# Layer 3's end, run as three stages in turn, against one walk in which shaping, convolutions and closing go side by side

## The chip, the cores and the metric

The kernel runs on one core of a Trainium2 chip. A core has TensorE (PE in the profile, with its weight loads shown apart as PEld), VectorE (DVE), ScalarE (ACT), GpSimd (POOL) and SyncE (SP), each with an instruction queue of its own; transfers are started from these queues and moved by 16 DMA engines. The metric is the device time of one execution in microseconds; a kernel's time is the median of its runs.

## What is computed

The network applies four layers to x of shape (4, 96, 56, 56) in float32: attention, a selective scan, a windowed mixture, and the layer of this change. Each layer's output is added to its input. Only the end of layer 3 matters here. Up to that point the layer has made `xz = in_proj(x)`, split in two halves of 192 channels, and four cumulative results `y` (rows, rows backwards, columns, columns backwards). The rest is, cut to its core:

```python
y1, y2 = y[:, 0], y[:, 1, :, ::-1]
y3, y4 = ...                      # the two column orders, turned back to row order
ys = y1 + y2 + y3 + y4            # each with its Ds added
mu, var = yn.mean(-1), yn.var(-1) # over 192 channels
yn = (yn - mu) / jnp.sqrt(var + 1e-05) * ln_g + ln_b
u = jnp.moveaxis(yn, -1, 1) * z   # z: second half of in_proj(x)
t = relu(bn(conv2d(u, c1_w)))                     # 1x1, 192 -> 384 channels
t = relu(bn(conv2d(t, c2_w, groups=384, pad=1)))  # 3x3, one filter per channel
t = conv2d(t, c3_w, c3_b)                         # 1x1, 384 -> 96 channels
s = relu(t.mean((2, 3)) @ se1_w.T + se1_b)
s = sigmoid(s @ se2_w.T + se2_b)
return t + t * s[:, :, None, None]
```

## The kernel before

An image has L = 3136 positions. They are taken in 7 chunks of 448 columns (8 image rows; `NCH`, `CH`), or in 28 groups of 112 positions (`KT`, `NKT`), four of which make a chunk. The 384 channels are three tiles of 128 (`NM`, index m). The four batches are called b.

`layer3` (L1516) first runs `into_layer3` and `cumulative`; neither is touched by the change, apart from the number of taps that `convolve` now gets with each tile. What follows them is the stage of this case. Its weights are loaded on SP's queue, the two batch norms are turned into scale and shift (L1543 and after), and then the loop over b (L1649 to L1659) does three things for one batch, and only then goes to the next batch:

1. Shaping, `gathered` (L1554). Per chunk it loads the four y tiles, 112 positions x 4 x 192 channels (L1565, L1571, all on SP's queue, three buffers of each), adds them and Ds on VectorE (L1575, L1576), normalises in `norm_rows` (L768: statistics L773 and L774, square root on ScalarE L776, reciprocal L778, subtract and scale L780, times gamma L784, plus beta L785), computes z by four matmuls with `wz` (L1581), multiplies (L1582), and turns the result by eight transposes (L1586) so that channels lie on partitions; ScalarE copies the halves into g (L1590).
2. Bottleneck, `convolve` (L386). It walks tiles and chunks; in one step it convolves chunk c of the tile before and fills chunk c of the next tile. A fill is two matmuls with c1 (L1601) and one ScalarE activation (L1605) into a padded image. The nine taps of the 3x3 filter are split: `on_pe` = 4 are matmuls with a diagonal matrix (L413, diagonals made at L399), which accumulate in PSUM; the other five are VectorE instructions on the same PSUM tile (L418); ScalarE's `ended` (L1611) writes the result to t2.
3. Closing. Seven times three matmuls with c3 (L1627) and an activation that also sums (L1628), then the mean (L1632, L1633), se1 (L1635, L1637), se2 with its sigmoid (L1639, L1641), and seven outputs `o` = t3 x gate + x (L1646), each written by a DMA from GpSimd's queue (L1647). x was loaded for the whole batch at L1594.

PSUM has eight banks: three for fills, turned halves and c3 (`op`), two for z (`oz`), three for the convolutions (`od`). The pools of SBUF are opened anew for every batch. The bottleneck's convolutions are issued `in_order`: the instructions of each engine run in the order in which the program writes them. Elsewhere a scheduler may move them.

Of the kernel before, what the change touches and what calls it, by code (L numbers as in the profile page):

```python
# [9 lines left out]
F32 = mybir.dt.float32  # L10
# [7 lines left out]
L = H * W  # L18
CH = 448
# [50 lines left out]
class Net:  # L70
# [315 lines left out]
    def convolve(self, tiles, two, sp, ps):  # L386

        nc = self.nc  # L390
        on_pe = 4
        for j in range(len(tiles) + 1):
            now = tiles[j] if j < len(tiles) else None
            old = tiles[j - 1] if j > 0 else None
            if now is not None:
                now["xp"] = two[j % 2]
                dg = now["dg"] = sp.tile([128, on_pe, 128], F32, name="dg")
                for k in range(on_pe):
                    nc.vector.tensor_scalar(  # L399
                        dg[:, k, :], self.ident, now["weights"][:, k : k + 1], None, ALU.mult  # L400
                    )
            for c in range(NCH):
                if old is not None:
                    xp, w = old["xp"], old["weights"]

                    def tap(k):
                        y = 8 * c + k // 3
                        return xp[:, y : y + 8, k % 3 : k % 3 + W]

                    p = ps.tile([128, 512], F32, name="d")  # L410
                    q = p[:, :CH].rearrange("p (h w) -> p h w", w=W)
                    for k in range(on_pe):
                        nc.tensor.matmul(q, old["dg"][:, k, :], tap(k), start=k == 0, stop=k == on_pe - 1)  # L413
                if now is not None:
                    now["fill"](c, now["xp"][:, 1 + 8 * c : 9 + 8 * c, 1 : W + 1])
                if old is not None:
                    for k in range(on_pe, 9):
                        nc.vector.scalar_tensor_tensor(q, tap(k), w[:, k : k + 1], q, ALU.mult, ALU.add)  # L418
                    old["ended"](c, q)

    def into_scan(self, xin, dram, orders):
# [7 lines left out]
        with ExitStack() as cx:  # L429
# [19 lines left out]
            def tile_of(pr, j):  # L449
# [46 lines left out]
                return dict(weights=cw[:, j, :], fill=fill, ended=ended)  # L496
# [594 lines left out]
    def into_layer3(self, xin, dram):  # L1091
# [4 lines left out]
        with ExitStack() as cx:  # L1096
# [19 lines left out]
            def tile_of(pr, j):  # L1116
# [41 lines left out]
                return dict(weights=cw[:, j, :], fill=fill, ended=ended)  # L1158
# [357 lines left out]
    def layer3(self, xin, xout, dram):  # L1516
# [4 lines left out]
        with ExitStack() as cx:  # L1521
            wp = cx.enter_context(tc.tile_pool(name="ow", bufs=1))
            ga = cx.enter_context(tc.tile_pool(name="og", bufs=1))
            ps = cx.enter_context(tc.tile_pool(name="op", bufs=3, space=PSUM))
            psz = cx.enter_context(tc.tile_pool(name="oz", bufs=1, space=PSUM))
            psd = cx.enter_context(tc.tile_pool(name="od", bufs=3, space=PSUM))
            wz = wp.tile([C, DI], F32, name="wz")
            nc.sync.dma_start(wz, self.d["l3_win"][:, DI : 2 * DI])

            lng, lnb, ds = (self.load_rows(wp, n) for n in ("l3_lnw", "l3_lnb", "l3_d"))  # L1530
            dsum = wp.tile([KT, DI], F32, name="dsum")
# [22 lines left out]
            def gathered(b, g, sp, ss):  # L1554

                xn = sp.tile([C, L], F32, name="xn")
                nc.sync.dma_start(xn, xs[b])
                for t0 in range(0, NKT, 4):
                    four = [KT, 4, DI]
                    yk = []  # L1560
                    for k in range(4):
                        y = ss.tile(four, F32, name=f"y{k}")
                        if k < 2:
                            src = ys[k][b, t0 * KT : (t0 + 4) * KT, :].rearrange("(t p) d -> p t d", p=KT)
                            nc.sync.dma_start(y, src)  # L1565
                        else:
                            for r in range(2):
                                src = ys[k][b].rearrange("(w h) d -> w h d", h=H)[
                                    :, 2 * t0 + r : 2 * t0 + r + 7 : 2, :
                                ]  # L1570
                                nc.sync.dma_start(y[r * W : (r + 1) * W], src)  # L1571
                        yk.append(y)
                    acc = yk[0]
                    for k in (1, 2, 3):
                        nc.vector.tensor_tensor(acc, acc, yk[k], ALU.add)  # L1575
                    nc.vector.tensor_tensor(acc, acc, spread(dsum, 4), ALU.add)  # L1576
                    self.norm_rows(acc, lng, lnb, ss)
                    z = psz.tile([KT, 4, 256], F32, name="z")
                    for i in range(4):
                        at = (t0 + i) * KT  # L1580
                        nc.tensor.matmul(z[:, i, :DI], xn[:, at : at + KT], wz, start=True, stop=True)  # L1581
                    nc.vector.tensor_tensor(acc, acc, z[:, :, :DI], ALU.mult)  # L1582
                    for dh in range(2):
                        p = ps.tile([128, 512], F32, name="pn")
                        for i in range(4):
                            nc.tensor.transpose(  # L1586
                                p[:96, i * KT : (i + 1) * KT], acc[:, i, 96 * dh : 96 * dh + 96],
                                self.ident[:KT, :KT],
                            )
                        nc.scalar.copy(g[:, dh, t0 * KT : (t0 + 4) * KT], p[:96, : 4 * KT])  # L1590

            def bottleneck(b, g, sp, s1, ss):
                x = s1.tile([C, L], F32, name="x")
                nc.sync.dma_start(x, xin[b])  # L1594
                t2 = s1.tile([128, NM, L], F32, name="t2")

                def tile_of(m):
                    def fill(c, dst):
                        p = ps.tile([128, 512], F32, name="pn")
                        for dh in range(2):  # L1600
                            nc.tensor.matmul(  # L1601
                                p[:, :CH], c1[:, dh, m * 128 : (m + 1) * 128],
                                g[:, dh, c * CH : (c + 1) * CH], start=dh == 0, stop=dh == 1,
                            )
                        nc.scalar.activation(  # L1605
                            dst, p[:, :CH].rearrange("p (h w) -> p h w", w=W),
                            AF.Relu, bias=s1h[:, m : m + 1], scale=s1c[:, m : m + 1],
                        )

                    def ended(c, p):  # L1610
                        nc.scalar.activation(  # L1611
                            t2[:, m, c * CH : (c + 1) * CH], flat(p),
                            AF.Relu, bias=s2h[:, m : m + 1], scale=s2c[:, m : m + 1],
                        )

                    return dict(weights=c2[:, m, :], fill=fill, ended=ended)

                two = self.padded(s1)
                with in_order(tc):
                    self.convolve([tile_of(m) for m in range(NM)], two, sp, psd)  # L1620
                t3 = s1.tile([C, L], F32, name="t3")
                sums = ss.tile([C, NCH], F32, name="sums")
                for c in range(NCH):
                    cs = slice(c * CH, (c + 1) * CH)
                    p = ps.tile([128, 512], F32, name="pn")
                    for m in range(NM):
                        nc.tensor.matmul(p[:C, :CH], c3[:, m, :], t2[:, m, cs], start=m == 0, stop=m == NM - 1)  # L1627
                    nc.scalar.activation(  # L1628
                        t3[:, cs], p[:C, :CH], AF.Identity, bias=c3b, accum_out=sums[:, c : c + 1]
                    )  # L1630
                mean = ss.tile([C, 1], F32, name="mean")
                nc.vector.tensor_reduce(mean, sums, AX.X, ALU.add)  # L1632
                nc.vector.tensor_scalar(mean, mean, 1.0 / L, None, ALU.mult)  # L1633
                p = ps.tile([128, 512], F32, name="pn")
                nc.tensor.matmul(p[: DI // 4, 0:1], se1, mean, start=True, stop=True)  # L1635
                h1 = ss.tile([DI // 4, 1], F32, name="h1")
                nc.scalar.activation(h1, p[: DI // 4, 0:1], AF.Relu, bias=se1b)  # L1637
                p = ps.tile([128, 512], F32, name="pn")
# [4 lines left out]
                for c in range(NCH):  # L1643
                    cs = slice(c * CH, (c + 1) * CH)
                    o = ss.tile([C, CH], F32, name="o")
                    nc.vector.scalar_tensor_tensor(o, t3[:, cs], gate, x[:, cs], ALU.mult, ALU.add)  # L1646
                    nc.gpsimd.dma_start(xout[b][:, cs], o)  # L1647

            for b in range(B):  # L1649
                g = ga.tile([96, 2, L], F32, name="g")  # L1650
                with ExitStack() as c2x:
                    sp = c2x.enter_context(tc.tile_pool(name="ob", bufs=1))
                    ss = c2x.enter_context(tc.tile_pool(name="os", bufs=3))
                    gathered(b, g, sp, ss)
                with ExitStack() as c2x:
                    sp = c2x.enter_context(tc.tile_pool(name="tb", bufs=2))
                    s1 = c2x.enter_context(tc.tile_pool(name="t1", bufs=1))
                    ss = c2x.enter_context(tc.tile_pool(name="ts", bufs=3))
                    bottleneck(b, g, sp, s1, ss)  # L1659
# [141 lines left out]
```

## Time and profile before

| | |
|---|---|
| median of 4 runs | 16304.19 us (16290.62 to 16332.49) |
| the profiled execution | 16290.62 us, span 16288.5 us |
| PE busy over the span | 13211.2 us (81%) |
| PEld | 8975.2 us (55%) |
| DVE | 13644.1 us (84%) |
| ACT | 12217.7 us (75%) |
| POOL | 7905.3 us (49%) |
| mean granted TensorE clock | 0.919 |
| the stage of the change | from about 15465 us to the end at 16288.5 us |

The page cuts the span into 40 slices; the stage is a little more than the last two of them. In these rows each digit is the busy share, or the granted clock, of one slice in tenths:

```profile
PE   8999977777777777777777678788888888888876
DVE  8666559999999999999998766678888888888866
ACT  0555449999999999999997255488888888888822
POOL 0000048888888888888886022133333333333300
PEclk7999989999999999999998588888999999999977
```

In the last two slices no engine is close to full, ScalarE is at two tenths and GpSimd at nought, and the clock is at seven tenths. A share of busy time over a slice of 407 us covers several batches' stages, so the stage has to be read in windows that follow these stages. The times of a group of instructions are recorded per instruction; a float32 matmul leaves two records.

### The profile page before, as it was taken

What the parts mean: (1) busy time and instruction counts of PE and PEld (TensorE: products, weight loads), DVE (VectorE), ACT (ScalarE), POOL (GpSimd) and SP (SyncE); (2) the same over time, 40 slices, a digit from 0 to 9 for tenths busy, and PEclk for the clock granted to TensorE, in tenths of its full rate; (3) what the DMA queues carried; (4) which work ended last, traced back from release to release, by engine and by line L of the source; (5) the groups of instructions that cost most, each with busy time, mean ns of one, the idle gap of its engine ahead of it and who ended that gap; (6) DMA issues with size and microseconds to landing.
All of it is one profiled execution on the core that took longest, in us unless ns stands there. A gap on an engine that the chain in (4) does not pass through costs nothing.

```text
span 16288.5 us, 501766 instructions
## 1 busy us (share of the span) xinstructions
PE 13211.2 (81%) x222032; PEld 8975.2 (55%) x222032; DVE 13644.1 (84%) x15363; ACT 12217.7 (75%) x15540; POOL 7905.3 (49%) x4079
## 2 busy tenths in 40 slices
PE   8999977777777777777777678788888888888876
PEld 4333336666666666666665555456666566666543
DVE  8666559999999999999998766678888888888866
ACT  0555449999999999999997255488888888888822
POOL 0000048888888888888886022133333333333300
PEclk7999989999999999999998588888999999999977
DMA  0000043333444433434445800221212221222122
GB/s 15 1 1 4 14 157 92 92 92 93 105 105 104 104 93 93 94 94 104 104 106 124 213 17 10 78 50 49 51 48 51 51 50 48 51 50 51 43 67 64
DMA packets 821406, 1152.54 MB, mean 71 GB/s; under 512 B 309360, under 2 KB 728720, under 8 KB 807456
## 3 DMA queue, kind: packets, MB, share of 16 engines
q1 hardware_dynamic: 759872, 1055.38, 26.5%
q10 hardware_dynamic: 53984, 45.77, 1.2%
q8 instruction: 1746, 28.61, 0.8%
q0 software_dynamic: 5376, 19.27, 0.4%
q14 instruction: 428, 3.51, 0.1%
HBM read 842.93 MB, written 277.18 MB: 69 GB/s over the span
## 4 chain that ended last, share of the span: by engine, by line
PE 34%; DVE 28%; ACT 21%; issue 11%; DMA 4%; POOL 1%; SPq 0%; ACTq 0%; DVEq 0%; POOLq 0%
DVE q L634 17%; PE q L1427 7%; ACT ht L659 5%; ACT e L622 4%; PE s L233 4%; PE d L413 3%; ACT phi L1375 3%; PE z L1367 3%; DVE w L1415 3%; PE acc L251 2%; PE m L196 2%; PE y L671 2%; ACT w L1383 2%; PE t L557 2%; PE t L650 2%
## 5 line engine op out<-in xcount | busy, mean ns | idle before, releaser
L614 POOL TENSOR_TENSOR q<-du,bm 128x1792 f32<-128x1792 f32 x1344 | 5348.7, 4026 | 3.1 <-DMA bm<-bc 3.1
L634 DVE TENSOR_TENSOR_SCAN q<-e,state,q 128x448 f32<-128x448 f32 x4608 | 4875.0, 1123 | 143.5 <-ACT e L622 137.3
L622 ACT ACTIVATE e<-dl,na 128x448 f32<-128x448 f32 x5376 | 3354.6, 640 | 173.2 <-DVE q L634 118.3
L671 PE MATMUL y<-ht,cd 128*32 128x64 f32 x75264 | 1839.2, 225 | 1468.9 <-ACT ht L659 1466.8
L650 PE MATMUL t<-ident,q 128*128 128x128 f32 x18816 | 2618.1, 293 | 94.0 <-issue 77.9
L1427 PE MATMUL q<-w,m 32*32 32x192 f32 x52224 | 2582.4, 348 | 118.3 <-DVE phi L1436 68.6
L650 PEld LDWEIGHTS t<-ident,q 128*128 128x128 f32 x18816 | 2382.7, 203 | 324.4 <-issue 200.9
L659 ACT COPY ht<-t 128x896 f32<-128x896 f32 x2688 | 2428.7, 904 | 91.5 <-PE t L650 60.7
L671 PEld LDWEIGHTS y<-ht,cd 128*32 128x32 f32 x75264 | 1402.3, 110 | 1947.8 <-ACT ht L659 1930.2
L1427 PEld LDWEIGHTS q<-w,m 32*32 32x32 f32 x52224 | 1878.0, 113 | 731.5 <-issue 162.2
L1436 DVE TENSOR_TENSOR phi<-q,phi 128x768 f32<-128x768 f32 x1632 | 1513.8, 953 | 547.3 <-PE q L1427 524.8
L1448 POOL TENSOR_TENSOR t<-t 128x384 f32<-128x384 f32 x408 | 407.2, 998 | 2999.5 <-DVE t L1447 2999.5
L1367 PE MATMUL z<-ad,sm 32*32 32x256 f32 x39168 | 1277.7, 391 | 397.0 <-ACT phi L1375 383.7
L1375 ACT COPY phi<-z 128x1536 f32<-128x1536 f32 x816 | 1164.9, 1428 | 536.2 <-PE z L1367 536.0
L241 ACT ACTIVATE e<-s 128x896 f32<-128x896 f32 (+1 forms) x1050 | 922.0, 915 | 846.9 <-PE m L196 505.0
L208 DVE TENSOR_REDUCE pm<-m 128x1 f32<-128x448 f32 (+1 forms) x1700 | 997.7, 618 | 618.9 <-PE m L196 574.2
L1415 DVE TENSOR_TENSOR w<-w,misc 128x3072 f32<-128x3072 f32 x408 | 1365.4, 3347 | 83.1 <-PE misc L1399 46.3
L1383 ACT ACTIVATE w<-phi,lntiny,w_k_rmask 128x3072 f32<-128x3072 f32 x408 | 1203.0, 2949 | 2.6
L1391 ACT ACTIVATE phi<-phi,w_k_nmask 128x3072 f32<-128x3072 f32 x408 | 1165.6, 2857 | 2.4
L196 PE MATMUL m<-ka,qa 32*128 32x448 f32 (+1 forms) x3400 | 1135.2, 614 | 8.6 <-DVE pm L208 7.5
L1367 PEld LDWEIGHTS z<-ad,sm 32*32 32x32 f32 x39168 | 709.8, 105 | 659.3 <-ACT phi L1375 469.3
L292 POOL DMA_DIRECT2D x<-xc x28 | 14.5, 517 | 2080.6 <-DVE xc L291 2079.6
(254 smaller groups left out, 18703.0 us busy)
## 6 DMA issues: line engine op xcount, KB each, us to landing
bm<-bc SPq DMA_DIRECT2D x896, 448.0 KB
cm<-cd SPq DMA_DIRECT2D x544, 186.0 KB
l1y<-out SPq DMA_DIRECT2D x672, 96.0 KB
l1y<-out SPq DMA_DIRECT2D x672, 72.0 KB
y<-l1y ACTq DMA_DIRECT2D x224, 168.0 KB
l3y<-y SPq DMA_DIRECT2D x1616, 23.2 KB
w<-l3cr SPq DMA_DIRECT2D x408, 48.0 KB
l3cr<-phi SPq DMA_DIRECT2D x408, 48.0 KB
```

The costliest lines, as they stand in the source:

```text
L614: nc.gpsimd.tensor_tensor(q, spread(s["du"][:, j, :], ng), s["bm"][g], ALU.mult)
L622: nc.scalar.activation(e[:, :CH], s["dl"][:, j, :], AF.Exp, scale=na[:, s["k"], j, n : n + 1])
L634: nc.vector.tensor_tensor_scan(a, e, a, first, ALU.mult, ALU.add)
L650: nc.tensor.transpose(flat(t)[:, 128 * c : 128 * c + 128], view(q, h * NC2 + c, [[NC, 128]]), self.ident,)
L659: nc.scalar.copy(t, flat(s["t", j, g, h])[:, : NC2 * 128])
L671: nc.tensor.matmul(s["y", j][r : r + 32, c // 4, 64 * half : 64 * half + 64], s["cd"][:, half, g, c, :], s["t", j, g, h][:, 128 * i + 64 * ...
L1367: nc.tensor.matmul(z[32 * b : 32 * b + 32, p, dh].rearrange("p n d -> p (n d)"), s["s"][ps_, dh, b, lo : lo + 32], st["ad"][ps_, dh, 8 * h ...
L1375: nc.scalar.copy(st["phi"][:, :, :, 8 * h : 8 * h + 8, :].rearrange("p a b n d -> p a b (n d)"), z.rearrange("p a b n d -> p a b (n d)"),)
L1383: nc.scalar.activation(w.rearrange("p a n d -> p (a n d)"), st["phi"].rearrange("p a b n d -> p (a b n d)"), AF.Sigmoid, bias=lntiny, scal ...
L1415: nc.vector.tensor_tensor(st["w"], st["w"], ut, ALU.mult)
L1427: nc.tensor.matmul(qp[bs, n, :DI], st["m"][bs, 4 * q + n, :], st["w"][bs, :, 4 * q + n, :], start=True, stop=True,)
L1436: nc.vector.tensor_tensor(ph, view(st[q], 0, [[256, 4], [32, 6], [1, 32]]), ph, ALU.mult)
```

## The change

Everything at the end of layer 3 is issued in one walk, in program order on every engine.

- `gathered(b)` becomes a generator that yields three times per chunk, and is cut into parts: `fetch` (loads, issued three chunks ahead at first and two ahead later; xn per chunk), `added`, `statistics` (with the square root on ScalarE), `normalised` (z matmuls, reciprocal, and the subtraction and scaling as four ScalarE Identity activations per chunk), `gated` (multiplication by z) and `turned`. Gamma is folded into the weight of z (`wg`), beta into a second one (`wz`), whose product with xn is accumulated by one 448-column matmul before four plain matmuls with the identity that turn the chunk.
- For the first batch, the additions stay on VectorE, and the loads of y1 and y3 go to ScalarE's queue. For the other three the additions are GpSimd's and all y loads SP's.
- `convolve` is called once, for all 12 tiles of the four batches, and calls `before()` ahead of a step and `beside()` behind it. `beside` advances the shaping of the next batches by one yield, `before` the closing of the batch before. So 13 slots of 7 steps are walked, 91 steps.
- `closing(b)` is a generator that starts in the 21(b+1)th step: one c3 chunk per step, then residual loads (seven on ScalarE's queue, in seven buffers `o`) with the mean, se1, se2 with the gate, one output per step.
- The taps on TensorE are 3, 2 and 3 for the three tiles instead of 4.
- PSUM: two banks for fills and c3 (`op`), two for z, one for the turned halves (`ot`), three for convolutions.

```diff
-    def convolve(self, tiles, two, sp, ps):
+    def convolve(self, tiles, two, sp, ps, before=lambda: None, beside=lambda: None):
...
             for c in range(NCH):
+                before()
                 if old is not None:
-                    xp, w = old["xp"], old["weights"]
+                    xp, w, on_pe = old["xp"], old["weights"], old["on_pe"]
...
                     old["ended"](c, q)
+                beside()
...
-            ps = cx.enter_context(tc.tile_pool(name="op", bufs=3, space=PSUM))
+            ps = cx.enter_context(tc.tile_pool(name="op", bufs=2, space=PSUM))
             psz = cx.enter_context(tc.tile_pool(name="oz", bufs=1, space=PSUM))
+            pst = cx.enter_context(tc.tile_pool(name="ot", bufs=1, space=PSUM))
             psd = cx.enter_context(tc.tile_pool(name="od", bufs=3, space=PSUM))
...
+            wg = wp.tile([C, DI], F32, name="wg")
+            nc.vector.tensor_tensor(wg, wz, lng[:C], ALU.mult)
+            nc.vector.tensor_tensor(wz, wz, lnb[:C], ALU.mult)
...
+            def fetch(b, c):
...
+                for k in range(4):
+                    y = ss.tile(four, F32, name=f"y{k}", bufs=3)
+                    queue = nc.sync if b > 0 or k % 2 == 0 else nc.scalar
...
+            def added(q):
+                y = q["ys"]
+                engine = nc.gpsimd if q["b"] > 0 else nc.vector
+                engine.tensor_tensor(y[0], y[0], y[1], ALU.add)
+                engine.tensor_tensor(y[2], y[2], y[3], ALU.add)
+                engine.tensor_tensor(y[0], y[0], y[2], ALU.add)
+                engine.tensor_tensor(y[0], y[0], spread(dsum, 4), ALU.add)
+
+            def statistics(q):
...
+                for i in range(4):
+                    nc.vector.bn_stats(st[:, i, :], acc[:, i, :])
+                    nc.vector.bn_aggr(mv[:, i, :], st[:, i, :])
+                rs = q["rs"] = ss.tile([KT, 4], F32, name="rs")
+                nc.scalar.activation(rs, mv[:, :, 1], AF.Sqrt, bias=self.eps[:KT])
+
+            def normalised(q):
...
+                for i in range(4):
+                    nc.tensor.matmul(
+                        z[:, i, :DI], q["xn"][:, i * KT : (i + 1) * KT], wg, start=True, stop=True
+                    )
+                nc.vector.reciprocal(rs, rs)
+                nm = ss.tile([KT, 4], F32, name="nm")
+                nc.vector.scalar_tensor_tensor(nm, mv[:, :, 0], -1.0, rs, ALU.mult, ALU.mult)
+                for i in range(4):
+                    nc.scalar.activation(
+                        acc[:, i, :], acc[:, i, :], AF.Identity,
+                        bias=nm[:, i : i + 1], scale=rs[:, i : i + 1],
+                    )
+
+            def gated(q):
+                acc = q["ys"][0]
+                nc.vector.tensor_tensor(acc, acc, q["z"][:, :, :DI], ALU.mult)
+
+            def turned(q):
...
+                for dh in range(2):
+                    p = pst.tile([128, 512], F32, name="tr")
+                    nc.tensor.matmul(
+                        p[:96, :CH], wz[:, 96 * dh : 96 * dh + 96], q["xn"], start=True, stop=False
+                    )
                     for i in range(4):
...
+                        nc.tensor.matmul(
+                            p[:96, i * KT : (i + 1) * KT], acc[:, i, 96 * dh : 96 * dh + 96],
+                            self.ident[:KT, :KT], start=False, stop=i == 3,
+                        )
+                    nc.scalar.copy(gs[b][:, dh, c * CH : (c + 1) * CH], p[:96, :CH])
+
+            def gathered(b):
+                qs = [fetch(b, c) for c in range(3)]
+                added(qs[0])
+                for c in range(NCH + 1):
+                    if c < NCH:
+                        statistics(qs[c])
+                    if c > 0:
+                        turned(qs[c - 1])
+                        if c + 2 < NCH:
+                            qs.append(fetch(b, c + 2))
+                    yield
+                    if c == NCH:
+                        return
+                    normalised(qs[c])
+                    if c + 1 < NCH:
+                        added(qs[c + 1])
+                    yield
+                    gated(qs[c])
+                    yield
...
+                return dict(weights=c2[:, m, :], on_pe=(3, 2, 3)[m], fill=fill, ended=ended)
...
+            def closing(b):
...
+                yield
                 for c in range(NCH):
...
+                    yield
+                os = []
+                def residual(c):
+                    o = ss.tile([C, CH], F32, name="o", bufs=7)
+                    nc.scalar.dma_start(o, xin[b][:, c * CH : (c + 1) * CH])
+                    os.append(o)
+                for c in range(NCH):
+                    residual(c)
...
+                    yield
+                    o = os[c]
+                    nc.vector.scalar_tensor_tensor(o, t3[:, cs], gate, o, ALU.mult, ALU.add)
                     nc.gpsimd.dma_start(xout[b][:, cs], o)
...
+            def ending():
+                for b in range(B):
+                    coming = closing(b - 1) if b > 0 else iter(())
+                    for _ in range(NM * NCH):
+                        next(coming, None)
+                        yield
+                yield from closing(B - 1)
+
+            ends = ending()
+            outputs = (x for b in range(1, B) for x in gathered(b))
+            with in_order(tc):
+                for _ in gathered(0):
+                    pass
+                self.convolve(
+                    [tile_of(b, m) for b in range(B) for m in range(NM)], two, sp, psd,
+                    lambda: next(ends, None), lambda: next(outputs, None),
+                )
+                for _ in ends:
+                    pass
```

## The prediction

> **What bounds the kernel now.** The change touches only the last 823 us of the span (15465 to 16288.5), so I read the windows of that stretch first, then its groups, the timeline, and windows of 3.41 us that lie on the clock's own grid.
>
> In the windows the columns after the bounds are length, busy time of PE, PEld, DVE, ACT, POOL, granted clock, DMA share and GB/s.
> ```profile
> 15465.00:15553.00 88.00, 32.73 (x116) 27.39 (x117) 66.00 (x161) 10.62 (x24) 0.78 (x8) 0.52 0.58 141
> 15553.00:15668.00 115.00, 110.47 (x295) 54.21 (x293) 74.55 (x115) 37.22 (x59) 0.52 (x1) 0.99 0.03 7
> 15668.00:15692.00 24.00, 2.87 (x8) 2.31 (x8) 9.42 (x19) 0.05 (x1) 3.09 (x7) 0.50 0.88 225
> 15692.00:15751.00 59.00, 26.69 (x105) 23.66 (x106) 57.23 (x135) 9.61 (x21) 0.00 (x0) 0.56 0.44 113
> ```
> Batch 0 is shaped in 88 us with DVE bound (clock 0.52), convolved and closed in 115 with PE full (0.99); batch 1 then waits 24 us for loads. The cycle, about 203 us, repeats four times. Over all of it PE is busy 573 us and DVE 568 of 823: most of what one does, the other stands beside.
>
> In the groups (busy, mean ns, idle before and its releasers) and two spots of the timeline:
> ```profile
> L418 DVE SCALAR_TENSOR_TENSOR d<-xp,w_l_c,d 128x448 f32<-128x448 f32 x420 | 287.4, 689 | 125.8 <-PE d L413 108.7 <-ACT t L1611 3.4
> L413 PE MATMUL d<-xp,dg 128*128 128x448 f32 x672 | 263.1, 538 | 0.0
> L1605 ACT ACTIVATE xp<-pn,bn_sh,bn_sc 128x448 f32<-128x448 f32 x84 | 61.1, 727 | 131.5 <-PE pn L1601 131.5
> ```
> ```profile
> 15777.70 3.66 DVE L418 SCALAR_TENSOR_TENSOR d<-xp,w_l_c,d 128x448 f32<-128x448 f32 x5 [0.86 <-PE d L413]
> 15776.88 0.73 ACT L1611 ACTIVATE t<-d,bn_sh,bn_sc 128x448 f32<-128x448 f32 x1 [1.46 <-DVE d L418]
> 15839.05 0.72 ACT L1611 ACTIVATE t<-d,bn_sh,bn_sc 128x448 f32<-128x448 f32 x1 [2.77 <-DVE d L418]
> ```
> Each 448-column f32 matmul is two records 0.376 us apart: 0.752. A step of four taps on PE plus fill is 6 x 0.752 = 4.51, while DVE's five taps take 3.66 (0.725 each): PE waits for nothing, DVE for PE.
> ```profile
> 4208.30:4211.71 3.41, 2.48 (x16) 1.71 (x14) 3.41 (x3) 3.37 (x6) 1.56 (x1) 1.00 0.70 152
> 4211.71:4215.12 3.41, 1.52 (x58) 1.27 (x59) 3.41 (x4) 3.41 (x6) 3.41 (x2) 0.99 0.00 0
> 4215.12:4218.54 3.42, 3.42 (x35) 3.09 (x36) 3.42 (x5) 2.66 (x6) 3.42 (x2) 0.51 0.08 19
> 15748.78:15752.19 3.41, 2.74 (x10) 2.22 (x11) 1.90 (x8) 1.06 (x2) 0.78 (x8) 0.50 0.06 11
> 15752.19:15755.60 3.41, 3.41 (x6) 1.50 (x5) 0.00 (x0) 0.73 (x1) 0.00 (x0) 0.50 1.00 258
> 15759.02:15762.43 3.41, 3.41 (x10) 1.71 (x9) 0.00 (x0) 1.45 (x2) 0.00 (x0) 1.00 0.00 0
> ```
> One window with PE 45% busy (1.52) halves the clock in the next; a cold window 80% busy (2.74) leaves it cold; after a full one (3.41) it is full again by 15759.
>
> **The change, part by part.** Program order holds on each engine, so I follow each queue; "step" is one chunk of one tile, 91 in all: 7 that only fill, 77 that fill and convolve, 7 that only convolve.
>
> Fewer taps on PE: (3,2,3) gives DVE 6, 7, 6. DVE's step is 6 x 0.725 = 4.35 or 5.05, PE's (with two fill matmuls) 3.76 or 3.01: DVE bounds a plain step where PE did.
>
> Shaping beside the steps. Per chunk on DVE: statistics 4 x (0.340 + 0.174) = 2.06, overlapped about 1.95; reciprocal and product 0.35 (L778 has 0.173 each); gating 0.96 (L1582, 0.941). Sum 3.26; 7 chunks over 3 tiles, 7.6 per tile. Removed: L780, L784, L785 and, for batches 1 to 3, the additions (L1575, L1576). GpSimd's additions: L1005 has 1.605 for 112x672 and 1.842 for 112x784, so 1.81 for 112x768, 7.2 per chunk, hidden behind the step and a half before their statistics; bare, 7.2 x 20 = 145. ACT's four Identities (112x192) lie between L945 (112x96, 0.363) and L1628 (96x448, 0.630): 0.46, nearer the first in size, 1.6 with their overlap, hidden under the step's taps; bare 1.6 x 21 = 34. PE gets four z matmuls (L1581: eight records in 2.77 at half clock, so about 1.3) and two 448-column ones for the folded lnb (1.5) per chunk: 2.8 x 7 = 20 a batch, under DVE's lead of 1.3 to 2.0 a step where no bubble stands. The folding itself is two products of 0.36 at the start.
>
> The new wait. In 19 of the conv steps (3 turns when the chunk's three steps fall so in a tile, else 2; only one in the last, at step 65) DVE's taps are followed by statistics, ACT's square root waits for these, and the copy of the first half of `turned` stands behind the root. With one bank for `tr`, PE's second half waits for that copy, and the next convolution is queued behind it on PE. From the end of statistics DVE is idle for root 0.30 (L776), copy 0.53 (L1590), second half 0.75 + 4 x 0.20 = 1.57 (two records each, 0.10 by L1030's ten in 1.01), next three taps 2.26, handovers 0.6: 5.3 us (4.6 with two taps). What is late next is the whole following step: its taps, `ended`, and the fill of the next tile. With root and copies in the other order it would be nothing; that is the lower bound, the upper one adds the half clock (below).
>
> Closing beside tile 2's steps. c3's third matmul needs `ended` of the step before and stands ahead of the next convolution, so the step is a chain: conv 2.26, gap 0.16, taps 4.35, `ended` 0.72, c3 0.75, handovers 0.25: 8.5. Shaping fits into it, bar about 5 per `turned`. It replaces 7 x 2.26 of bare closing per batch.
>
> Queues. SP gets the y and xn loads two chunks ahead and only them; each waits for its buffer, and nothing else stands behind it. POOL's output DMAs (L1647, 0.51) stand behind its additions, with seven `o` buffers nobody waits for them. Residual loads: 7 issues at 0.31 to 0.34 (L834) on ACT, which stands until y loads in flight land (1.55 MB at 225 GB/s, 6.9 us); mostly hidden, 3 us x 3. With all cover gone 7 x 3.
>
> First batch: nine y loads move to ACT's queue ahead of the bn roots. SP keeps the rest, weights between y parts; DVE's bn work stands between the additions. Chunk 0's sums I put at 29.5 us (now its statistics start at 23.7); bounds 23.7 and 24 + 2 x 6.9 = 38. Then a chunk is a chain over ACT, PE and DVE: root 0.3, copy 0.53, second half at half clock 3.1, copy 0.53, four Identities 1.6, gating 0.96, statistics 1.95, six handovers of 0.2: 10.2 (the copies on ACT are 8.72 apart at present, and DVE's own work, additions 3.9 + 3.26, is 7.2). Four such, two of 9.2 where the turn is missing or early, a last turn of 6 and 7 to the first fill: 102 (now 85.5, from 15465 to the first fill). The 7 fill-only steps: 10.5 + two turns x 4.7 = 20.
>
> Sum at full clock: seven steps of 4.35 (30.5), 5.05 (35.4) or 8.5 (59.5) per tile, shaping 7.6, bubbles, outputs (L1646, 0.70 each, steps 11 to 17 of the next batch), ACT's 3:
> - batch 0: 30.5 + 7.6 + 2 x 5.3 = 48.7; 35.4 + 7.6 + 2 x 4.6 = 52.2; 59.5 + 2 x 5 = 69.5; together 170
> - batch 1 (three turns in its first tile): 30.5 + 7.6 + 15.9 + 2 = 56; 35.4 + 7.6 + 9.2 + 2.8 = 55; 69.5 + 3; together 184
> - batch 2 (two, three and one): 51; 60; 59.5 + 5 + 3 = 67.5; together 178
> - batch 3 (no shaping left): 33; 38; 59.5 + 3; together 134
> - start 102, fills 20, tail 23: last `ended` 0.7, c3 1.0, its copy 0.8, seven residual issues 2.3, mean, se1 and table load 2.9, seven outputs 4.8 (without today's waits for three buffers, 10.4 in L1646's row), and from the last output to the span's end the 10.5 that lie there now (16277.98 to 16288.5)
>
> Total 811, 12 below 823.
>
> The clock. In each bubble PE stands still for 4 to 5 us; a window is then under 45% busy, wherever the grid lies, and the next is cold, till one is full. A cold window loses at most 1.7 on PE's chain; one or two of them: 2.5, x 19 = 47 (bounds 0 and 3.4 x 19 = 65). Closing steps have PE 6.0 of 8.5 busy, the last seven 4.5: about 18 more. 811 + 65 = 876, +53.
>
> The Trainium skill ("TensorE: Matmul & The Clock Gate", What's actually happening) gives a full clock after one busy window and half after an idle one. Here 45% busy counted as idle and 80% as not busy; by the page alone few windows are idle and the sum would be some 821.
>
> The skill ("SBUF — State Buffer", Who interferes with whom) speaks against the change: a VectorE instruction with two SBUF inputs shuts out a GpSimd instruction reading SBUF and the reverse. No row here shows it; by it 21 outputs could each wait for one addition, at most 21 x 1.81 = 38.
>
> The sum stands against the profiled run's 16290.62 (span 16288.5); the median shown, 16304.19, lies 13.57 above it. Forecast 16304 + 53 = 16357 us.
>
> **Rivals.**
> - The clock holds, PE's idle pieces being split by fills and halves of `turned`: 811, so 16292. For: before, full windows recover at once. Against: the 45% row.
> - Overlap works and the bubbles do not form, the copies running ahead of the roots. Without 19 x 5 and with closing steps at 5.5 (taps 4.35 and 7.6 / 7 of shaping; 7 x 4 x 3.0) 811 - 95 - 84 = 632; half of that gain gives 721, so 16202. For: busy sums, DVE and PE about 122 each per batch. Against: order on ACT and PE. It decides if over a third of the bubbles vanish.
> - More loss: ACT stands for residual loads (21 in place of 9) and both clock bounds at their top (65 + 18): 876 + 12 + 18 = 906, 16387; with the first sums at 38 besides, 16396. For: the bounds above have no row that cuts them; against: they must all come at once.
>
> **How the numbers follow.** Forecast 0.54, clock holds 0.21, overlap 0.16, more loss 0.09. Time 16357. The forecast's own range is 16318 to 16395 (39 below, 38 above: the clock's 65 going down to half or all bounds up by 18, the start 29.5 moving by 6 to 8.5, ACT's residual loads by 12). 0.2% is 32.6 us, what a measurement here can tell. Slower: 0.47 of the forecast and 0.09; same: 0.07 of the forecast and 0.18 of the clock case; faster: its other 0.03 and 0.16. The range reaches down into the overlap case, 16250, and up to the last, 16396, and the runs' own spread above it: 16405.
>
> **What would show it.** DVE idle before L418's line, released by PE, some 5 us 19 times; PE released by ACT's copy of `tr`; steps of 8.5 us in tile 2; clock about 0.7 over the stage; first fill near +102; GpSimd far from busy. Wrong if L418's idle is under 60 us beyond tile 2, if the clock stays above 0.9 (then 16292), or if steps near 5 us show in `turned` steps (overlap).

## The result, and the profile after

The changed kernel takes 16353.48 us (median of 50 runs, 16302.53 to 16411.98), the kernel before 16327.64 (75 runs, 16279.15 to 16383.61). The ratio is 1.0017, interval 1.0012 to 1.0023: slower by 28 us (the medians lie 26 apart), less than 0.2% and more than nothing.

The profiled run of the changed kernel has a span of 16380.9 us, 92 more than before. Most of that isn't the change: the last instruction of the cumulative part on VectorE (L1447 before, L1448 after, both followed by 4.2 us to the first load on SyncE) lies at 15460.8 before and at 15529.8 after, though the instructions up to there are the same. From here on "the stage" is what follows: 823.5 us before, 846.9 after. The difference, 23.4, fits the ratio of the many runs.

These are the page's slices, busy tenths and clock, of the changed kernel; its stage is the last two:
```profile
DVE  8666559999999999999998766678888888888865
ACT  0465449999999999999997255488888888888732
POOL 0000039888888888888886022133333333333321
PEclk7899889999999999999998588889999999999888
```
GpSimd has work in them now, and VectorE has less than before. One window over the stage (length, then busy PE, PEld, DVE, ACT, POOL, clock, DMA share, GB/s) and four groups:
```profile
15534.00:16381.00 847.00, 587.86 (x1752) 320.56 (x1752) 505.31 (x955) 232.28 (x436) 166.69 (x120) 0.82 0.26 64
```
```profile
L418 DVE SCALAR_TENSOR_TENSOR d<-xp,w_l_c,d 128x448 f32<-128x448 f32 x532 | 366.1, 689 | 263.9 <-PE d L413 248.2
...
L1698 PE MATMUL pn<-t,w_l_c 128*96 128x448 f32 x168 | 85.7, 629 | 59.9 <-ACT t L1682 59.9
...
L1633 PE MATMUL tr<-xn,wz 96*96 96x448 f32 x112 | 72.3, 736 | 119.7 <-ACT g L1641 119.7
...
L1590 POOL TENSOR_TENSOR y<-y,y 112x768 f32<-112x768 f32 x21 | 38.0, 1810 | 259.7 <-DMA y<-l3y 115.8 <-DVE st L1600 79.2 <-DVE d L418 62.2
```
VectorE's busy time fell from 567.6 to 505.3 us, but it stood 248 us in front of its taps for TensorE (109 before). TensorE itself stood 119.7 us for the copy of a turned half (L1641) and 59.9 us for `ended` (L1682). These are the two waits of the prediction.

One turned step, in the timeline (start, duration, engine):
```profile
15659.20 0.91 PE L1633 MATMUL tr<-xn,wz 96*96 96x448 f32 x2
...
15659.23 4.31 DVE L418 SCALAR_TENSOR_TENSOR d<-xp,w_l_c,d 128x448 f32<-128x448 f32 x6
...
15659.95 0.93 PE L1637 MATMUL tr<-ident,y 112*96 112x112 f32 x8
...
15665.49 0.30 ACT L1603 ACTIVATE rs<-mv,eps 112x4 f32<-112x4 f32 x1 [1.20 <-DVE mv L1601]
15665.69 0.51 ACT L1641 COPY g<-tr 96x448 f32<-96x448 f32 x1
...
15666.25 1.81 PE L1633 MATMUL tr<-xn,wz 96*96 96x448 f32 x2 [5.37 <-ACT g L1641]
...
15667.85 1.70 PE L1637 MATMUL tr<-ident,y 112*96 112x112 f32 x8
...
15669.34 3.21 PE L413 MATMUL d<-xp,dg 128*128 128x448 f32 x6
...
15672.59 4.32 DVE L418 SCALAR_TENSOR_TENSOR d<-xp,w_l_c,d 128x448 f32<-128x448 f32 x6 [7.20 <-PE d L413]
```
The first half is ready on TensorE at 15660.9, but its copy is made at 15665.69, behind the square root, which waits for the statistics behind the taps. TensorE stands 5.37 us, then goes on at half rate (1.81 us for the two records that took 0.91 in the first half, 1.70 for the eight that took 0.93), and VectorE gets its next taps after 7.20 us. Windows on the clock's grid around this step show the clock:
```profile
15660.76:15664.17 3.41, 0.13 (x2) 0.00 (x0) 3.27 (x7) 0.60 (x1) 0.00 (x0) 0.99 0.00 0
15664.17:15667.59 3.42, 1.34 (x2) 0.68 (x3) 1.12 (x6) 0.83 (x3) 0.00 (x0) 0.50 0.00 0
15667.59:15671.00 3.41, 3.41 (x12) 2.33 (x11) 0.00 (x0) 0.53 (x1) 0.00 (x0) 0.52 0.11 18
15671.00:15674.41 3.41, 3.41 (x13) 1.90 (x12) 1.75 (x3) 0.31 (x1) 0.00 (x0) 1.00 0.83 237
```
An empty window is followed by two at half rate, of which the second is full.

And c3 steps of the last batch, TensorE's and VectorE's rows:
```profile
16349.70 1.40 PE L1698 MATMUL pn<-t,w_l_c 128*96 128x448 f32 x2 [3.73 <-ACT t L1682]
16350.89 3.75 PE L413 MATMUL d<-xp,dg 128*128 128x448 f32 x6
16354.48 1.67 PE L1698 MATMUL pn<-t,w_l_c 128*96 128x448 f32 x4
```
```profile
16344.57 4.31 DVE L418 SCALAR_TENSOR_TENSOR d<-xp,w_l_c,d 128x448 f32<-128x448 f32 x6 [5.86 <-PE d L413]
...
16354.75 4.31 DVE L418 SCALAR_TENSOR_TENSOR d<-xp,w_l_c,d 128x448 f32<-128x448 f32 x6 [5.86 <-PE d L413]
```
c3's third matmul (the last two records) waits 3.73 us for `ended`, the convolution follows at half rate, and VectorE stands 5.86 us in a step of 10.18.

### The profile page after: what moved, and what is told of

Read it like the earlier page. It is cut to its first block, busy times and chain, and to the rows that moved or that the text cites. A ratio compares the mean times of both kernels' runs of the same rounds, so it can differ in the third digit from the quotient of the medians.

```text
span 16380.9 us, 501944 instructions
## 1 busy us (share of the span) xinstructions
PE 13291.5 (81%) x222144; PEld 8976.3 (55%) x222144; DVE 13583.5 (83%) x15237; ACT 12258.0 (75%) x15650; POOL 8054.4 (49%) x4139
## 4 chain that ended last, share of the span: by engine, by line
PE 34%; DVE 28%; ACT 21%; issue 12%; DMA 4%; POOL 1%; SPq 0%; ACTq 0%; DVEq 0%; POOLq 0%
DVE q L635 16%; PE q L1428 8%; ACT ht L660 5%; ACT e L623 4%; PE s L233 4%; PE z L1368 3%; ACT phi L1376 3%; DVE w L1416 2%; PE acc L251 2%; PE m L196 2%; PE y L672 2%; PE d L413 2%; PE t L558 2%; PE t L651 2%; ACT phi L1392 2%
```

## The experiments

Each is the changed kernel with one edit, or with some of these edits together. "Stage" is read as above from each run's own profile, since the part ahead of it varies from run to run by more than some of the effects; the ratio is to the kernel before, with its 95% interval. Each stage is one profile: in the six runs that share the changed kernel's code up to the first fill (the first c1 matmuls), that fill begins 91.3 to 93.5 us after the stage's start, and in two that share another start (e3 and e6) at 80.9 and 85.5, so differences of a few us between stages say little.

**Turned ahead of the taps (e1).** `gathered` yields twice as often, and the turned part is advanced between fill and taps.
```diff
+                amid()
                 if old is not None:
                     for k in range(on_pe, 9):
...
-                    if c < NCH:
-                        statistics(qs[c])
                     if c > 0:
                         turned(qs[c - 1])
...
                     yield
+                    if c < NCH:
+                        statistics(qs[c])
+                    yield
```


> Turned is issued between a step's fill and its taps, the statistics stay behind the taps; nothing else moves. The stage is 846.9 us in the changed kernel (from the last L1448 plus 4.2 us to the end). My theory (VectorE stands 5.4 to 8.2 us after each of 19 turned steps, since the second half waits for a copy that stands behind the square root): these waits fall to under 1.5 us each outside the c3 steps, 14 x 6.5 = 91 less, stage about 750. Rival 1 (the waits only move to another place, the fill or the clock): 15 to 40 less, stage 810 to 830. Rival 2 (VectorE's own work sets the time, its waits are cover for GpSimd's additions and the loads): no more than 10 less.

Stage 758.7, 88.2 less; ratio 0.9968 (0.9956 to 0.998). Outside the c3 steps VectorE's waits after turned steps are 0 to 1.5 us, as I expected, but for one of 4.99: there seven residual loads, which hold ScalarE for 3.17 us, now stand ahead of the copy. Its whole wait for L413 fell from 248.2 to 140.6. Rivals 1 and 2 fall. It had a price that I had not seen: in the first batch, where nothing lies between, the same edit puts both copies ahead of the root on ScalarE, and the first fill came 106.6 us after the stage's start (91.3 in the changed kernel). Without these 15 the gain is 103.

**c3 behind the convolution (e2).** `before()` is called behind the convolution's matmuls.
```diff
             for c in range(NCH):
-                before()
                 if old is not None:
...
                         nc.tensor.matmul(q, old["dg"][:, k, :], tap(k), start=k == 0, stop=k == on_pe - 1)
+                before()
                 if now is not None:
```


> The closing's piece of a step (c3 among it) is issued behind the convolution's matmuls instead of ahead of them. My theory (c3's third matmul waits for ended of the step before and holds back the next convolution, so 28 steps are a chain of 8.4 to 10.2 us): the steps fall to about 6, bound by ended 0.72, c3 0.75, fill 1.5, convolution 2.26 and handovers; 28 x 3 = 84 less, stage about 763. Rival (the steps are long because the clock is halved in them, the order being harmless): steps stay over 8, under 20 less.

Stage 751.6, 95.3 less; ratio 0.9951 (0.9934 to 0.9968). The last batch's c3 steps now have this form:
```profile
16228.31 2.42 PE L412 MATMUL d<-xp,dg 128*128 128x448 f32 x6
16230.57 2.42 PE L1698 MATMUL pn<-t,w_l_c 128*96 128x448 f32 x6
16232.82 2.42 PE L412 MATMUL d<-xp,dg 128*128 128x448 f32 x6
```
They repeat every 4.51 us (six matmuls of 0.752) instead of 10.18, with no wait on TensorE. In the other batches a c3 step without a turn takes 6.0 to 7.3 (8.4 to 10.2 in the changed kernel). The rival, that the clock alone made them long, falls: the order did, and the clock added up to 1.8 us on top.

**Two banks for the turned halves (e3).**
```diff
-            pst = cx.enter_context(tc.tile_pool(name="ot", bufs=1, space=PSUM))
-            psd = cx.enter_context(tc.tile_pool(name="od", bufs=3, space=PSUM))
+            pst = cx.enter_context(tc.tile_pool(name="ot", bufs=2, space=PSUM))
+            psd = cx.enter_context(tc.tile_pool(name="od", bufs=2, space=PSUM))
```


> Two PSUM banks for the turned halves, two instead of three for the convolutions; order as in the changed kernel. My theory (one bank is what makes the second half wait for the copy): PE's wait before L1633 falls from 119.7 us to under 25, VectorE's before the taps by 19 x 6 = 110, stage about 740. Rival 1 (the order of root and copy on ScalarE alone costs it, or the third convolution bank is needed): under 25 less, or a new wait of PE's convolutions on ScalarE's ended of 30 us and more.

Stage 723.9, 123.0 less; ratio 0.9943 (0.9926 to 0.9961). A turned step on TensorE:
```profile
15592.22 0.91 PE L1633 MATMUL tr<-xn,wz 96*96 96x448 f32 x2
15592.97 0.93 PE L1637 MATMUL tr<-ident,y 112*96 112x112 f32 x8
15593.74 0.92 PE L1633 MATMUL tr<-xn,wz 96*96 96x448 f32 x2
15594.50 0.93 PE L1637 MATMUL tr<-ident,y 112*96 112x112 f32 x8
15595.26 2.43 PE L413 MATMUL d<-xp,dg 128*128 128x448 f32 x6
```
Both halves and the next convolution follow without a stop, and over the stage TensorE no longer waits before L1633 (119.7 us in the changed kernel). The order of root and copy is as it was, so the wait needs the single bank as well as that order: e1 removes it by the one, this run by the other. The third bank for convolutions had a use, as the first rival said it might:
```profile
L413 PE MATMUL d<-xp,dg 128*128 128x448 f32 x448 | 215.3, 619 | 35.5 <-ACT t L1682 35.4
```
TensorE's convolutions now wait 35.4 us for `ended` (12.7 in the changed kernel; c3's wait stays, 65.2). The stage fell all the same, and outside the c3 steps VectorE's waits behind turned steps are 0 to 0.42 us. This buys 35 us more than e1, 27 of them ahead of the first taps: the first fill comes at 80.9 us after the stage's start, 10 earlier than in the changed kernel, where e1 has it 15 later.

**TensorE kept busy (e4).** Six matmuls into the idle z banks behind the first half.
```diff
                     nc.scalar.copy(gs[b][:, dh, c * CH : (c + 1) * CH], p[:96, :CH])
+                    if dh == 0 and b > 0:
+                        idle = psz.tile([KT, 4, 256], F32, name="z")
+                        for _ in range(6):
+                            nc.tensor.matmul(
+                                idle[:, 0:2, :224], self.ident[:96, :KT],
+                                q["xn"].rearrange("p (a b) -> p a b", a=2), start=True, stop=True,
+                            )
```


> As the changed kernel, with six 448-column matmuls (4.5 us at full clock) into the unused z banks between the two halves of each turned chunk of batches 1 to 3; their result is read by nobody. My theory of the clock (each stop of PE is followed by one or two cold windows, 2.5 us a time): the clock over the stage rises from 0.84 to over 0.90 and the stage falls by 20 to 45, to 802 to 827. Rival (the cold windows lie where nobody waits for PE): clock up, time within 8 of 847. Third case (the extra matmuls reach past the stop): slower by up to 19 x 2.

```profile
15519.50:16342.30 822.80, 649.65 (x2004) 343.63 (x2004) 507.70 (x955) 232.34 (x436) 166.65 (x120) 0.90 0.27 66
```
Stage 822.8, 24.1 less, with 62 us more of TensorE's busy time; clock 0.90 instead of 0.82; ratio 1.0003 (0.999 to 1.0016). (The expectation has 0.84 for the changed kernel; over the whole stage it is 0.82.) From VectorE's first taps on, the run is 33 us shorter, 25 of them in tiles 0 and 1; ahead of the first taps it is 9 longer, 7 of them in the steps that only fill, where two turned chunks stand. The cold windows after the stops cost time of their own: 33 us for those that this edit fills, where I had charged 47 for all.

**Both waits removed (e5: e1 and e2; e6: e3 and e2).**

> The first two experiments' edits together: turned between fill and taps, c3 behind the convolution. Alone they took 88.2 and 95.3 us off the stage of 846.9. My theory (two separate waits): both come off, 846.9 - 88 - 95 = 664, give or take 15, since five of the 19 turned steps are c3 steps too. Rival (a common cause, such as the cold clock, which either removes): 720 to 750, little more than either alone.

> Two banks for the turned halves (alone 123.0 less: 723.9) and c3 behind the convolution (alone 95.3 less). My theory: 723.9 - 95 = 629, give or take 15, some 195 under the kernel before's 823.5, so a ratio near 0.988. Rival (common cause): 700 or more.

e5: stage 679.5, ratio 0.9915 (0.9898 to 0.9932), half a us above what I gave; e6: stage 641.8, ratio 0.9877 (0.9861 to 0.9893), within what I gave. The two gains add up within 13 to 16 us; that the turned c3 steps are in both is the likely reason, not a shown one. There is no common cause.

**The first batch (e7, e8).** `engine = nc.gpsimd` for all batches; `queue = nc.sync` for all loads.

> As the changed kernel, but the first batch's additions on GpSimd too. A chunk of the first batch is a chain of 10.2 us over ScalarE, TensorE and VectorE, and four additions on GpSimd take 7.2 beside it: by my reading the chain hardly grows; only the first chunk's sums come 3.4 us later, with the wait for the batch norms' constants on VectorE taken out of them. First fill at 91.3 after the stage's start now; I expect 89 to 96. Rival (VectorE's additions shorten the start as the change's words say): over 100.

> As the changed kernel, but all y loads on SyncE's queue. The changed kernel's first sums are complete 22.1 us after the stage's start, held by the second half of y2, which SyncE issues at 16.2 behind 14 weight loads, and by the batch norms' work on VectorE. I expect sums at 18 to 26 and the first fill at 88 to 96. Rival (the second queue is what starts the loads early): sums at 28 or later and the first fill at 97 or later.

e7: first fill at 97.4 us, stage 857.1, ratio 1.0027 (1.0017 to 1.0038). VectorE's additions are worth some 6 us up to the first fill and 10 in all: more than I gave them, less than the rival. (The interval of the ratio overlaps that of the changed kernel, 1.0012 to 1.0023, here and in e8; the first fill shows more than the runs' times.) e8: first fill at 86.4, stage 843.4, ratio 1.0012 (1.0001 to 1.0023): the first sums are complete at 19.9 us (22.1 in the changed kernel), so the second queue for the first loads doesn't shorten the start; by these profiles it costs 3 to 5 us. In the changed kernel SyncE issues its weight loads from 15534.9 to 15550.0, while ScalarE issues its nine, and the batch norms' constants arrive 17.3 us after the stage's start; in e8 it is 11.5, in the kernel before 8.7.

**Taps (e10).** `on_pe=(4, 4, 4)` in the changed kernel.

> As the changed kernel, with four taps on TensorE for all tiles, as in the kernel before. By my chain a turned step and a c3 step lose a tap of 0.72 (two in tile 1) on VectorE and gain a matmul of 0.75 on TensorE in the same chain: even. The plain steps (30 of the 84) go from 4.35 or 5.05 plus shaping to 4.51 with the matmuls: 0 to 0.5 less each. Expect the stage at 835 to 860 against 846.9. Rival (VectorE's work bounds, so fewer taps there shorten everything): 800 or less. Rival (TensorE's work bounds): 875 or more.

Stage 816.9, 30.0 less; ratio 0.9999 (0.9988 to 1.0009). A miss: I had it even. VectorE's busy time fell to 434.1, TensorE's rose to 649.3, the clock to 0.88. One stop in a turned step:
```profile
15668.95 1.80 PE L1633 MATMUL tr<-xn,wz 96*96 96x448 f32 x2 [3.32 <-ACT g L1641]
```
It is 3.32 us long instead of 5.37: TensorE, with a matmul more in each step, comes to it 1.3 us later against VectorE's taps, and VectorE has a tap less (0.7). By tile (start of the first taps to the next tile's) the time went from tile 1 (16 less over four batches, five taps on VectorE instead of seven) and tile 2 (15 less); tile 0 stays within 2. VectorE's full weight, 0.72 a tap, does not come back either: 532 - 420 = 112 taps, 71 us of its busy time, bring 30. And the clock rose with TensorE's work: how much of the 30 us is the clock's and how much the taps', no run separates.

**Residual loads (e11).** `nc.sync.dma_start(o, ...)` in `closing`.

> As the changed kernel, with the closing's seven residual loads on SyncE's queue. My prediction charged them with 3 us for each of three batches and 2.3 at the end. Expect the stage 5 to 11 less, 836 to 842. Rival (ScalarE's stand lies where it had nothing to do): within 3 of 846.9.

Stage 845.1, 1.8 less, no more than such profiles vary by; ratio 1.0023 (1.0012 to 1.0033). The rival holds. In the changed kernel ScalarE issues the first batch's from 15842.76 to 15847.74, while it has nothing to do: the fill that it works on next ends on TensorE at 15847.7.

**Additions on VectorE for all batches (e12).** `engine = nc.vector`.

> As the changed kernel, with the additions of all batches on VectorE; the 21 sets of four take 3.85 there. My theory: GpSimd's additions are wholly hidden now, and on VectorE they stand in plain steps or c3 steps: of 21 x 3.85 = 81 those in c3 steps (6 or 7 sets) lie in VectorE's waits, so 45 to 65 more, stage 890 to 915. Rival (GpSimd's additions are late in some steps or shut VectorE out, so moving them gives back part): 860 to 885. Rival (VectorE has room everywhere): under 860.

Stage 894.0, 47.1 more; ratio 1.004 (1.0027 to 1.0052). GpSimd's additions are covered, and moving them there is worth 47 us of the change.

**The best version (e9).** e6 with all y loads on SyncE's queue and `on_pe=(3, 3, 2)`.

> The sixth experiment's kernel (stage 641.8) with the first batch's y loads on SyncE's queue and taps on TensorE (3, 3, 2) instead of (3, 2, 3). There tile 2's steps are bound by TensorE at 6.0 us (three taps, fill, c3: eight matmuls of 0.752) with VectorE at 4.3, and tile 1's by VectorE at 5.0 plus shaping. My theory: tile 2's 21 steps fall to about 5.4, tile 1's 28 by 0.4, the start by 4: 12 + 11 + 4 = 27 less, stage 605 to 630. Rival (handovers set these steps, not the work): within 6 of 638.

```profile
15488.00:16087.60 599.60, 509.35 (x1752) 280.81 (x1752) 501.35 (x955) 229.01 (x436) 168.64 (x120) 0.94 0.37 91
```
Stage 599.6, ratio 0.986 (0.9845 to 0.9876), 5 us below the range that I gave. VectorE is busy 501 of the 600 us, and 79.5 of the 600 go by up to the first fill. Against e6 it is 42 us. By tile (start of the first taps to the next tile's), over four batches, tile 1 gave 27 (I expected 11), tile 2 only 5 (12), tile 0 4, and the time up to the first taps 6 (4, within what the start varies by). So it was tile 1 that took the stage below the range, while tile 2 gave less than I expected of it; the rival, that handovers set these steps, falls for tile 1 and is not far off for tile 2.

## Why the prediction came out as it did

The forecast was 53 us slower by one mechanism; it is 23 by the stage and 28 by the runs, by that mechanism. The time, 16353 beside a forecast of 16357, flatters it, since the median of the kernel before moved up by 23 us with more runs: that closeness is luck. In parts of the stage, the time up to VectorE's first taps is 115 us (about 122 by the forecast), the tiles take 710 (731 with the clock's 65), the tail 22 (23). Point by point:

- *The new wait* was right in its place, its cause and its count. The trace has 19 turned steps with a wait ahead of their following taps, 14 outside the c3 steps with 5.41 to 8.38 us, 94.7 together. At full clock I had 5.3 and 4.6; e4, where the windows behind the first stops stay warm, has 4.93 and 4.18 there. The lower bound I gave, nothing with another order, is what e1 shows there.
- *c3 as a chain* was right: 8.4 at full rate in the trace (15780.51 to 15788.92, 8.5 forecast), up to 10.18 with the clock. e2 shows the order as cause.
- *The clock* was mis-sized, and is the larger error. Tiles 0 and 1 of all batches take 424.0 us, 394 by my sum at full clock: 30 over 14 stops, 2.1 each, where I put 2.5 (e4, with its matmuls in the stops, comes to 398.7 there). Tile 2 takes 285.9 against 272 (of which 9 were the residual loads, which e11 puts at 2): so some 21 there instead of 30. Together about 51 of 65; that all of it is the clock's is not shown, e4 gets back 33 of it by filling the stops. Over the stage the clock is 0.82, where I had said about 0.7. The rival in which the clock holds falls with the 0.50 and 0.52 windows above; the one with more loss falls with these sizes.
- *The start* was the other error: first sums 22.1 us after the stage's start (29.5 forecast, bounds 23.7 and 38, so below the lower bound), first fill at 91.3 (102). The nine loads on the second queue, which began 3.5 us ahead of SyncE's first, are not the reason: e8 has the first sums at 19.9 without them. In both runs SyncE's first y load stands ahead of the weights, in the kernel before 8.4 us behind its first weight; whether that is the reason, no run shows. The chain of 10.2 per chunk held: statistics start at 15563.37, 15573.66 and 15584.01, 10.3 apart.
- *Residual loads*: 3 x 3 charged, and 1.8 found by e11, which isn't clear of nothing.
- *Taps*: I took fewer taps on TensorE as even in the chains. e10 shows 30 us against them, with the waits in place and the clock's part in it. With four taps the change would have made no difference that these runs can tell.
- *GpSimd's additions*: 1810 ns (1.81 forecast), hidden, as said; e12 has their price. The four Identities take 0.535 each, 1.85 together (1.6).
- *Overlap* (rival two) was what the rearrangement could give, and did not: e6 and e9 reach 642 and 600, about its 632, once the two waits are out.
- Of the rules weighed: by the clock page of the Trainium skill ("TensorE: Matmul & The Clock Gate", What's actually happening) I had a sum of 821 us. At the 19 turned steps, the full-rate window that the first cold one follows has TensorE busy for 0.00 to 0.53 us of 3.41 in nine cases, which the page's idle window covers, and for 1.01 to 1.71 in ten, which its words leave open. So what it misses here is not small. The lock that "SBUF — State Buffer", Who interferes with whom, states does show, at instructions that I had not thought of (rows in the last section). The outputs, for which I had named at most 38 us, take 648 to 681 ns, and in the changed kernel none of the 28 runs beside an addition.

## What to carry to other kernels

When stages are woven into one program order, look on each engine for the instruction that waits for this step's last result and stands ahead of the next step's first: here one copy behind a square root and one matmul behind an activation turned overlap into lockstep; removing them gave 123 (10 of it in a shorter start) and 95 us. One more buffer for the handed-over tile, or the same piece called a few lines later, removed each. Choose the split of work between engines again once such waits are gone: with them in place, fewer taps on TensorE cost 30 us (e10), and without them another split of the same number of taps on TensorE, with the other queue, gave 42 (e9). What four taps would give without the waits, no run here shows.

## What the runs showed of the hardware

- The share of busy TensorE below which the next window is halved lies between two fifths and a little over half of a window, and not sharply. Two pairs in the changed kernel:
```profile
15582.25:15585.66 3.41, 1.81 (x11) 0.88 (x9) 2.42 (x8) 0.86 (x2) 0.00 (x0) 0.99 1.06 269
15585.66:15589.08 3.42, 2.26 (x6) 1.34 (x7) 1.50 (x6) 0.71 (x2) 0.00 (x0) 0.50 0.65 137
...
15790.47:15793.88 3.41, 1.42 (x4) 0.32 (x2) 3.31 (x5) 1.29 (x2) 0.00 (x0) 1.00 0.00 0
15793.88:15797.29 3.41, 3.24 (x9) 1.72 (x10) 0.21 (x1) 0.84 (x3) 0.00 (x0) 1.00 0.00 0
```
1.81 us busy of 3.41 were followed by a cold window, 1.42 were not; in the kernel before, 1.52 were. On this grid every full-rate window of the stage with less than 1.4 us was followed by a cold one, none with more than 1.85 was, and between these both occur.
- The c3 steps of the last batch fell into step with the clock: 10.18 us is close to three windows (10.24), with one nearly empty (0.30 to 0.62 us busy), one cold and full, one warm in each step. Without the wait they take 4.51; with the wait and no cold window such steps take 8.41 in the first batch.
- VectorE and GpSimd shut each other out, and the one that starts first goes on. VectorE's 112 x 4 product for `nm`, both inputs in SBUF, takes 0.16 us as a rule; 8 of 28 were started beside an addition of GpSimd and took 0.18 to 1.77, the longest here:
```profile
15928.47 1.77 DVE L1615 SCALAR_TENSOR_TENSOR nm<-mv,rs 112x4 f32<-112x4 f32 x1
```
```profile
15928.42 1.81 POOL L1591 TENSOR_TENSOR y<-y,y 112x768 f32<-112x768 f32 x1 [1.71 <-DMA y<-l3y]
```
Each of the eight ends when the addition ends. `dg` (L398, 0.28) took up to 1.90 in the same way. In e12, with no additions on GpSimd, the longest are 0.164 and 0.283. Over the stage it adds up to 28 x (0.358 - 0.162) + 32 x (0.361 - 0.277) = 8 us of VectorE. The taps (L418), one input of which is in PSUM, stay at 0.69. The other way round, in e9 four additions started beside an output, and took 2.26 to 2.29 us instead of 1.81:
```profile
15756.19 0.68 DVE L1732 SCALAR_TENSOR_TENSOR o<-t,gate,o 96x448 f32<-96x448 f32 x1
```
```profile
15756.25 2.29 POOL L1592 TENSOR_TENSOR y<-y,y 112x768 f32<-112x768 f32 x1
```
- The part of the span ahead of the stage, with the same instructions, ended between 15460.8 and 15529.8 us in these profiles. A difference of 25 us in a single run's time says nothing about the stage; the stage's own length does.
